# A two-layer graph network on Trainium2: row transfers in two parts of 67 and 61 rows, edge features from a 17-row copy, attributes in groups of prime size

## The chip, the cores and the metric

The kernel runs on one NeuronCore of a Trainium2 chip. The metric is device time in microseconds (us) of one execution, and lower is better. One execution was also profiled; engines are named as in the profile: PE is TensorE (matmuls), PEld its weight loads, DVE is VectorE, ACT is ScalarE, POOL is GpSimd, SP is SyncE.

## What is computed

There are 6250 nodes with 160 float32 features (64 scalars and 32 vectors of three components) and 200,000 edges, sorted by their destination node. Each of two layers gathers the features of every edge's source node, multiplies them with attributes of the edge (`edge_attr_4`, called `sh` in the kernel), sums the products by destination node, applies small dense weights to the sums, adds a residual and normalizes each node's row. Layer 1 also has a small network on ten further features of each edge (`edge_attr_10`, called `ea` in the kernel).

```python
def _L0_gnn_ref(x, sh, W1, ..., edge_index):
    ss, vv = (s[src], v[src])
    ...
    m = jnp.concatenate([out0, out1.reshape(-1, 3 * MUL1)], axis=1)
    m_agg = jax.ops.segment_sum(m, dst, num_segments=n)
    ...
    return x + jax.nn.relu(h)

def _L1_gnn_ref(node_input, node_attr, edge_src, edge_dst, edge_attr, edge_length_embedded, ...):
    h = jax.nn.relu(edge_length_embedded @ W_fc1 * (1.0 / np.sqrt(N_BASIS))) * RELU_GAIN
    w = h @ W_fc2 * (1.0 / np.sqrt(N_RADIAL))
    ...
    m0 = w0 * y0 * e0
    ...
    s0 = jax.ops.segment_sum(m0, edge_dst, num_segments=N) * inv
    ...
    return jnp.concatenate([out0, out1.reshape(N, 3 * MUL1)], axis=1)

x = _layernorm(x + _L0_gnn_ref(x, edge_attr_4, ...), axis=-1)
x = _layernorm(x + _L1_gnn_ref(x, node_vec1, src, dst, edge_attr_4, edge_attr_10, ...), axis=-1)
```

## The kernel before

The edges are cut into 391 chunks of 512 (`NCH`, `CH`), each four times 128 edges, and the nodes into 49 blocks of 128 (`NB`; the last has 106). `windowed` runs `sums` once for each layer. Since the edges are sorted, the destinations of one chunk lie in a narrow window of nodes (one window up to chunk 312, `HALF`; from there each chunk has two, one for either half of the partitions), and their sum is a small matmul into PSUM, added at the window's place in `acc`, an array in SBUF with a column for every node. The order of the chunks (`ORDER`, and its inverse `POS`) mixes those before and behind 312 in runs of eight and four.

The schedule is written out by hand, as a software pipeline. At step t each stage works on the chunk that stands `lag` places back in `ORDER`. The stages of layer 1, and then those of layer 0, are:

```python
stages = [(load, 0), (onehot, 1), (hidden, 1), (add, 4), (message, 2), (matmuls, 3)]
parts = [(fetch_base, 3), (project_last, 5), (residual_last, 6), (deviation, 7), (sent, 8)]
...
stages = [(load, 0), (onehot, 1), (add, 3), (matmuls, 2)]
```

- `load` issues four indirect DMAs of 128 rows on POOL (L206, `g<-in_x` in layer 0, `g<-ytab` in layer 1); a chunk's rows go into one of eight `g` buffers (`GRING`), and POOL waits until the matmuls of the chunk eight places earlier have read theirs. These are the gathers. Nothing else of weight runs on POOL.
- `load` also starts, in layer 1, the features of four chunks at every fourth chunk: two loads on SP (L342) of 10 rows each into partitions 0 to 9 and 64 to 73 of `et` or `early`, by turns. The `hidden` stage of the same chunk reads them one step later.
- The attributes come in groups of up to 32 chunks (`GROUPS`, 13 in each layer). Eight places before a group's first chunk, `attributes` issues four loads of up to 32 rows on SP into the tile `raw` (L368), one behind the other; where a group has fewer than 32 chunks, VectorE first sets `raw` to zero (L366). `turn` transposes the tile on VectorE (L374) at the group's first chunk. `raw` has one buffer.
- `onehot` compares each edge's destination with the window's nodes on VectorE (L381) and multiplies by the attributes into `S` (L385).
- In layer 1, `hidden` computes the network's hidden units (L394 on PE into `ph`, L397 on ACT into `h`), and `message` its outputs (L407 on PE into `pw`) and the products with the gathered rows (L410 and L415 on VectorE into `m`).
- `matmuls` multiplies `S` with the gathered rows, or with `m`, into `ab` in PSUM (L427); `add` transposes the result and adds it to `acc` on VectorE (L444 to L449).

When the last chunk of a node block is through (at position `CLOSE[b]`, at least three apart), the block's own steps follow, each some places later. In layer 0: `fetch` loads its rows of x (`xt`, SP, L486), `project` multiplies the sums with the weights (L461), `rectify` (`rl` on ACT, L497), `residual`, `deviation` (`sd` on ACT) and `normed` make the new rows, `turned`, `kept` (`xT` on ACT) and `linear` multiply them with layer 1's input weights, and `written` sends one result to `ytab` (ACT, L533), from which layer 1 gathers, and another to `btab` (SP, L537). In layer 1: `fetch_base` loads the block's rows of `btab` (`base`, SP, L486), and `project_last` (L548), `residual_last` (L553), `deviation` and `sent` finish it, the last with the write to `out` (SP, L559). All these transfers have 128 rows of 640 bytes, and go from SP or ScalarE; the gathers go from POOL through a queue of their own.

Of the kernel before, what the change touches and what calls it, by code (L numbers as in the profile page):

```python
# [18 lines left out]
P = 128  # L19
# [4 lines left out]
J = 4  # L24
# [20 lines left out]
PREPARE = 8  # L45

# [49 lines left out]
def floor_of(c):  # L96

    done = [b for b in range(NB) if CLOSE[b] < POS[c]]
    near = [b for b in done if (b >= LATE) == (c >= HALF)] or [b for b in done if b < LATE]
    return P * (max(near) + 1) if near else 0  # L100

# [110 lines left out]
def windowed(ctx: ExitStack, tc: tile.TileContext, x, srcs, rel, low, ident, iota, early, ahead, ea, sh, avec,  # L212
# [10 lines left out]
    btab = dram.tile([N, D], F32, name="btab")  # L223

# [87 lines left out]
    def sums(layer, table, gp, hp):  # L312
        with ExitStack() as s:
# [13 lines left out]
            def load(c):  # L327
                if layer or c not in ahead:
                    G[c] = gathered(nc, gp.tile([P, J, D], F32, name="g"), srcs, table, c)
                else:  # L330
                    G[c] = ahead.pop(c)
                if c % 4 == 0 and layer:

                    if POS[c] % 8 >= 4:
                        et = xp.tile([P, 2, CH], F32, name="et")
                    else:
                        et = early.rearrange("p a j d -> p (a j d)")
                        et = et[:, :2 * CH].rearrange("p (s e) -> p s e", s=2)
                    ET[c // 4] = et
                    for i in range(2):  # L340
                        if c + 4 <= NCH:
                            nc.sync.dma_start(et[64 * i:64 * i + 10, :, :],  # L342
                                              ea[:, c * CH:(c + 4) * CH].rearrange("f (s i e) -> f s i e", s=2, i=2)[:, :, i, :])
                        else:
                            for k in range(c + i, NCH, 2):
                                nc.sync.dma_start(et[64 * i:64 * i + 10, (k - c) // 2, :], ea[:, k * CH:(k + 1) * CH])
                for first, n in GROUPS:
                    if fetched[first] == POS[c]:
                        attributes(first, n)


            GROUPS = sorted(((a, min(32, end - a)) for begin, end in ((0, HALF), (HALF, NCH))
                             for a in range(begin, end, 32)), key=lambda g: POS[g[0]])
            fetched, last = {}, -2
            for first, n in GROUPS:
                fetched[first] = max(0, POS[first] - 8, last + 2)
                last = POS[first]

            def group(c):
                return c - (c - (c >= HALF) * HALF) % 32  # L360

            def attributes(first, n):

                raw = RAW[first] = hp.tile([P, 512], F32, name="raw")
                if n < 32:
                    nc.vector.memset(raw, 0.0)  # L366
                for q in range(4):
                    nc.sync.dma_start(raw[32 * q:32 * q + n, :],  # L368
                                      sh[first:first + n, 32 * q:32 * q + 32, :].rearrange("c p f -> c (p f)"))
# [6 lines left out]
            def onehot(c):  # L376
                if group(c) == c:
                    turn(c)
                w = width(c)
                oh = bank[:, :J * W].rearrange("p (j n) -> p j n", n=W)  # L380
                nc.vector.tensor_tensor(oh[:, :, :w], iota[:, None, :w].to_broadcast([P, J, w]),  # L381
                                        rel[:, c, :, None].to_broadcast([P, J, w]), op=ALU.is_equal)
                S[c] = ring[:, POS[c] % 3]
                attr = SH[group(c)][:, :, c - group(c)].rearrange("p (j k) -> p j k", j=J)
                nc.vector.tensor_tensor(S[c][:, :, :, :w], oh[:, :, None, :w].to_broadcast([P, J, 4, w]),  # L385
                                        attr[:, :, :, None].to_broadcast([P, J, 4, w]), op=ALU.mult)
# [68 lines left out]

            def projected(name, pool, weights, b):
                r = rows(b)
                po = T[name, b] = pool.tile([P, D], F32, name=name)
                for g in range(5):
                    lhs = acc[:, g, b * P:b * P + r]  # L460
                    nc.tensor.matmul(po[:r], lhs, weights[:, g, :], start=(g == 0), stop=(g == 4))  # L461
# [22 lines left out]
            def rows_of(name, table, b):  # L484
                t = T[name, b] = np_.tile([P, D], F32, name=name)
                nc.sync.dma_start(t[:rows(b)], table[b * P:b * P + rows(b), :])  # L486
# [41 lines left out]
            def written(b):  # L528
# [4 lines left out]
                nc.scalar.dma_start(ytab[b * P:b * P + r, :], y[:r])  # L533
# [3 lines left out]
                nc.sync.dma_start(btab[b * P:b * P + r, :], base[:r])  # L537
# [19 lines left out]
            def sent(b):  # L557
                normed("o", b)
                nc.sync.dma_start(out[b * P:b * P + rows(b), :], T.pop(("o", b))[:rows(b)])  # L559

            if layer:
                stages = [(load, 0), (onehot, 1), (hidden, 1), (add, 4), (message, 2), (matmuls, 3)]
# [5 lines left out]
            for t in range(max(CLOSE.values()) + 16):  # L568
                for f, lag in stages:
# [6 lines left out]
                if not layer:  # L576
                    for k in range(2 * t, min(2 * t + 2, 5)):
                        clear(k)
                if not layer and t == PREPARE:
# [394 lines left out]
```

## Time and profile before

| | |
|---|---|
| median of 4 runs | 4925.79 us |
| lowest and highest | 4915.60 and 4934.29 us |
| the profiled execution | 4930.84 us |
| its span (first to last instruction) | 4928.7 us |
| mean granted TensorE clock | 0.75 of full speed |
| PE busy | 2998.7 us, 61% |
| PEld busy | 2238.9 us, 45% |
| DVE busy | 2158.0 us, 44% |
| ACT busy | 376.0 us, 8% |
| POOL busy | 2965.7 us, 60% |
| gathers' queue (q0): packets, MB, share of 16 engines | 150144, 256.45, 19.5% |
| transfers from SP (q1) | 40702, 31.55, 2.2% |
| transfers from ScalarE (q10) | 7164, 4.80, 0.3% |

No engine is busy all the time. Layer 0 takes roughly the first 2264 us of the span, layer 1 the rest from about 2307 us; both have the same 391 chunks of four gathers, so the two layers take 1.43 and 1.65 us for each gather on average. The share of a queue is the time that its packets took, as a share of the time of 16 DMA engines, each with a ring of its own: 100% would be all 16 at work throughout. In a view of the instructions, a bracket or the last column gives the idle time just before, and after the arrow what ended it.

### The profile page before, as it was taken

What the parts mean: (1) busy time and instruction counts of PE and PEld (TensorE: products, weight loads), DVE (VectorE), ACT (ScalarE), POOL (GpSimd) and SP (SyncE); (2) the same over time, 40 slices, a digit from 0 to 9 for tenths busy, and PEclk for the clock granted to TensorE, in tenths of its full rate; (3) what the DMA queues carried; (4) which work ended last, traced back from release to release, by engine and by line L of the source; (5) the groups of instructions that cost most, each with busy time, mean ns of one, the idle gap of its engine ahead of it and who ended that gap; (6) DMA issues with size and microseconds to landing.
All of it is one profiled execution on the core that took longest, in us unless ns stands there. A gap on an engine that the chain in (4) does not pass through costs nothing.

```text
span 4928.7 us, 42324 instructions
## 1 busy us (share of the span) xinstructions
PE 2998.7 (61%) x12714; PEld 2238.9 (45%) x12715; DVE 2158.0 (44%) x6948; ACT 376.0 (8%) x747; POOL 2965.7 (60%) x3137
## 2 busy tenths in 40 slices
PE   2333433443444454455677877777777877778777
PEld 1333323333334343444455555555555555555555
DVE  3222222222323333333455555555555556556556
ACT  2000000000000000001000000000000001001000
POOL 5666666666666666664555555565555556555553
PEclk7656656666666666667788888888888888888888
DMA  2222222222222222222221222121222222222221
GB/s 65 64 57 58 62 64 64 60 66 62 68 64 66 63 68 64 68 70 55 57 57 53 59 57 57 54 62 53 57 61 56 59 59 62 59 54 60 57 58 38
DMA packets 198245, 295.60 MB, mean 60 GB/s; under 512 B 59270, under 2 KB 140668, under 8 KB 198010
## 3 DMA queue, kind: packets, MB, share of 16 engines
q0 software_dynamic: 150144, 256.45, 19.5%
q1 hardware_dynamic: 40702, 31.55, 2.2%
q10 hardware_dynamic: 7164, 4.80, 0.3%
q8 instruction: 107, 1.75, 0.1%
q14 instruction: 128, 1.05, 0.1%
HBM read 280.57 MB, written 12.00 MB: 59 GB/s over the span
## 4 chain that ended last, share of the span: by engine, by line
PE 39%; another core or an unknown queue 35%; DVE 13%; issue 10%; POOL 2%; ACT 1%; DMA 0%; DVEq 0%; ACTq 0%; SPq 0%; POOLq 0%
PE ab L427 22%; PE pw L407 10%; DVE m L415 3%; PE ph L394 3%; DVE S L385 3%; PE ph L461 2%; POOL g L206 2%; DVE acc L449 1%; DVE m L410 1%; PE bank L548 1%; DVE ab L447 1%; DVE ab L444 1%; DVE bank L381 1%; DVE ab L445 1%
## 5 line engine op out<-in xcount | busy, mean ns | idle before, releaser
L206 POOL DMA_INDIRECT g<-ytab,srcs x1564 | 1480.6, 947 | 1127.7 <-issue 441.6
L206 POOL DMA_INDIRECT g<-in_x,srcs x1556 | 1472.8, 947 | 761.1 <-issue 431.9
L427 PE MATMUL ab<-g,S 128*128 128x160 f32 (+1 forms) x3744 | 737.1, 399 | 818.9 <-issue 453.5
L427 PE MATMUL ab<-m,S 128*128 128x320 f32 (+1 forms) x3760 | 1094.2, 496 | 96.0 <-DVE acc L449 85.3
L427 PEld LDWEIGHTS ab<-g,S 128*128 128x128 f32 (+1 forms) x3744 | 655.2, 264 | 906.5 <-issue 465.6
L407 PE MATMUL pw<-fc,h 100*128 100x192 f32 x3128 | 733.0, 383 | 481.2 <-DVE m L415 376.7
L407 PEld LDWEIGHTS pw<-fc,h 100*128 100x128 f32 x3128 | 604.3, 221 | 713.9 <-issue 349.7
L427 PEld LDWEIGHTS ab<-m,S 128*128 128x128 f32 (+1 forms) x3760 | 700.0, 221 | 367.7 <-issue 200.8
L447 DVE STREAM_TRANSPOSE ab<-ab 128x160 f32<-128x160 f32 x470 | 169.4, 360 | 1301.2 <-remote 1036.3
L385 DVE TENSOR_TENSOR S<-bank,sh 128x384 f32<-128x384 f32 (+2 forms) x782 | 431.0, 551 | 642.3 <-remote 280.6
L415 DVE TENSOR_TENSOR m<-g,pw 128x192 f32<-128x192 f32 x1564 | 474.5, 344 | 0.0
L410 DVE TENSOR_TENSOR m<-pw,g 128x256 f32<-128x256 f32 x782 | 327.2, 418 | 287.8 <-remote 157.4
L397 ACT ACTIVATE h<-ph 100x512 f32<-100x512 f32 x391 | 229.7, 596 | 2278.5 <-remote 1054.0
L449 DVE TENSOR_TENSOR acc<-acc,ab 128x120 f32 (+2 forms) x940 | 261.4, 278 | 246.2 <-remote 130.9
L381 DVE TENSOR_TENSOR bank<-iota,rel 128x96 f32<-128x96 f32 (+2 forms) x782 | 199.2, 255 | 176.5 <-remote 82.8
L461 PE MATMUL ph<-wb,acc 128*128 128x160 f32 (+1 forms) x490 | 128.0, 436 | 242.7 <-DVE acc L449 140.8
L461 PEld LDWEIGHTS ph<-wb,acc 128*128 128x128 f32 (+1 forms) x490 | 111.9, 291 | 259.5 <-DVE acc L449 100.2
L445 DVE STREAM_TRANSPOSE ab<-ab 32x160 f32<-32x160 f32 x470 | 165.6, 352 | 16.2
L444 DVE STREAM_TRANSPOSE ab<-ab 128x160 f32<-128x160 f32 x470 | 167.1, 356 | 10.7 <-issue 5.8
L525 PE MATMUL pl<-wn,xT 128*128 128x320 f32 (+1 forms) x98 | 52.1, 622 | 136.2 <-issue 70.0
L394 PE MATMUL ph<-early,fc 10*100 10x512 f32 x392 | 118.9, 668 | 1.8 <-issue 1.7
L394 PE MATMUL ph<-et,fc 10*100 10x512 f32 x390 | 108.5, 628 | 1.2 <-issue 1.2
(80 smaller groups left out, 731.9 us busy)
## 6 DMA issues: line engine op xcount, KB each, us to landing
g<-ytab,srcs POOLq DMA_INDIRECT x1564
g<-in_x,srcs POOLq DMA_INDIRECT x1556
raw<-in_sh SPq DMA_DIRECT2D x88, 64.0 KB
early<-in_ea SPq DMA_DIRECT2D x98, 40.0 KB
xt<-in_x SPq DMA_DIRECT2D x48, 80.0 KB
ytab<-y ACTq DMA_DIRECT2D x48, 80.0 KB
btab<-base SPq DMA_DIRECT2D x48, 80.0 KB
et<-in_ea SPq DMA_DIRECT2D x96, 40.0 KB
```

Source lines behind the costliest of these rows:

```text
L206: nc.gpsimd.indirect_dma_start(out=g[:, j, :], out_offset=None, in_=table, in_offset=bass.IndirectOffsetOnAxis(ap=srcs[:, c, j:j + 1], axi ...
L381: nc.vector.tensor_tensor(oh[:, :, :w], iota[:, None, :w].to_broadcast([P, J, w]), rel[:, c, :, None].to_broadcast([P, J, w]), op=ALU.is_e ...
L385: nc.vector.tensor_tensor(S[c][:, :, :, :w], oh[:, :, None, :w].to_broadcast([P, J, 4, w]), attr[:, :, :, None].to_broadcast([P, J, 4, w]) ...
L394: nc.tensor.matmul(ph[:, i, :], fc1[g:g + 10, :], ET[c // 4][g:g + 10, c % 4 // 2, :], start=True, stop=True)
L397: nc.scalar.activation(H[c], H["p"][:, c % 2, :].rearrange("f (p j) -> f j p", j=J), AF.Relu, scale=FC_SCALE)
L407: nc.tensor.matmul(pw[:, j, :], h[:, q + j, :], fc2, start=True, stop=True)
L410: nc.vector.tensor_tensor(mq[:, :, :, 0:64], pw[:, :, 0:128].rearrange("p j (a u) -> p j a u", a=2), y[:, :, None, 0:64].to_broadcast([P, ...
L415: nc.vector.tensor_tensor(mq[:, :, a, 64:160].rearrange("p j (d u) -> p j d u", d=3), y1, pw[:, :, None, w:w + 32].to_broadcast([P, 2, 3, ...
L427: nc.tensor.matmul(ab[:, :n], one[h * i:h * i + h, j, :, :], t[h * i:h * i + h, j, :], start=(j == 0), stop=(j == J - 1), skip_group_check ...
L447: nc.vector.transpose(tr, blocks[:, 0])
L449: nc.vector.tensor_tensor(v, v, tr[:, :, :width(c)], op=ALU.add)
L461: nc.tensor.matmul(po[:r], lhs, weights[:, g, :], start=(g == 0), stop=(g == 4))
```

## The change

Most transfers of SP and ScalarE that run beside the gathers get a prime number of rows.

- The rows of a node block (`xt`, `base`, `btab`, `out` and `ytab`) are sent by a new helper, `sent_rows`, in two transfers, the first of 67 rows (`LEADS`) and the second of 61. The last block (106 rows) and the blocks that close within the last eight chunks keep one; 46 of 49 are split.
- The features are read from a copy in DRAM, `etab`, with 17 rows (`ROWS`): the ten of `ea` and the first seven again. Layer 0 makes it in eight stretches of the columns, each with two DRAM-to-DRAM transfers of 10 and 7 rows from SP, at its steps 32, 64 and so on to 256. Layer 1's loads bring all 17 rows into `et` (the matmuls still read ten of them), in a stage of its own that runs three chunks (`LEAD`) ahead of `load`.
- The attributes come in 15 groups of 31, 23, 19 or 17 chunks (`SIZES`). A group's four loads no longer follow each other but are issued one for each chunk, from twelve places ahead of its first chunk (or, where the group before is still in `raw`, as soon as that allows, then all at once if fewer than four places are left). Every group's `raw` is first set to zero.

```diff
--- before.py
+++ after.py
@@ -44,6 +44,12 @@
 GRING = 8
 PREPARE = 8
 
+LEADS = 67
+ROWS = 17
+SIZES = (31, 31, 31, 31, 31, 31, 23, 23, 23, 19, 19, 19, 31, 31, 17)
+COPIES = 8
+LEAD = 3
+
 
 def expected(node, sign):
 
@@ -98,6 +104,15 @@
     done = [b for b in range(NB) if CLOSE[b] < POS[c]]
     near = [b for b in done if (b >= LATE) == (c >= HALF)] or [b for b in done if b < LATE]
     return P * (max(near) + 1) if near else 0
+
+
+def group(c):
+
+    first = 0
+    for n in SIZES:
+        if c < first + n:
+            return first, n
+        first += n
 
 
 def windows(c):
@@ -221,6 +236,7 @@
     dram = ctx.enter_context(tc.tile_pool(name="dram", bufs=1, space=bass.MemoryType.DRAM))
     ytab = dram.tile([N, D], F32, name="ytab")
     btab = dram.tile([N, D], F32, name="btab")
+    etab = dram.tile([ROWS, NCH * CH], F32, name="etab")
 
     acc = const.tile([P, 5, NW], F32, name="acc")
     bank = ctx.enter_context(tc.tile_pool(name="bank", bufs=1, space=PSUM)).tile([P, 512], F32, name="bank")
@@ -329,44 +345,43 @@
                     G[c] = gathered(nc, gp.tile([P, J, D], F32, name="g"), srcs, table, c)
                 else:
                     G[c] = ahead.pop(c)
-                if c % 4 == 0 and layer:
-
-                    if POS[c] % 8 >= 4:
-                        et = xp.tile([P, 2, CH], F32, name="et")
+                for first, n in GROUPS:
+                    for q in range(4):
+                        if POS[c] == fetched[first] + (q if POS[first] >= fetched[first] + 4 else 0):
+                            attributes(first, n, q)
+
+            def features(c):
+                if c % 4:
+                    return
+
+                if POS[c] % 8 >= 4:
+                    et = xp.tile([P, 2, CH], F32, name="et")
+                else:
+                    et = early.rearrange("p a j d -> p (a j d)")
+                    et = et[:, :2 * CH].rearrange("p (s e) -> p s e", s=2)
+                ET[c // 4] = et
+                for i in range(2):
+                    if c + 4 <= NCH:
+                        nc.sync.dma_start(et[64 * i:64 * i + ROWS, :, :],
+                                          etab[:, c * CH:(c + 4) * CH].rearrange("f (s i e) -> f s i e", s=2, i=2)[:, :, i, :])
                     else:
-                        et = early.rearrange("p a j d -> p (a j d)")
-                        et = et[:, :2 * CH].rearrange("p (s e) -> p s e", s=2)
-                    ET[c // 4] = et
-                    for i in range(2):
-                        if c + 4 <= NCH:
-                            nc.sync.dma_start(et[64 * i:64 * i + 10, :, :],
-                                              ea[:, c * CH:(c + 4) * CH].rearrange("f (s i e) -> f s i e", s=2, i=2)[:, :, i, :])
-                        else:
-                            for k in range(c + i, NCH, 2):
-                                nc.sync.dma_start(et[64 * i:64 * i + 10, (k - c) // 2, :], ea[:, k * CH:(k + 1) * CH])
-                for first, n in GROUPS:
-                    if fetched[first] == POS[c]:
-                        attributes(first, n)
-
-
-            GROUPS = sorted(((a, min(32, end - a)) for begin, end in ((0, HALF), (HALF, NCH))
-                             for a in range(begin, end, 32)), key=lambda g: POS[g[0]])
+                        for k in range(c + i, NCH, 2):
+                            nc.sync.dma_start(et[64 * i:64 * i + ROWS, (k - c) // 2, :], etab[:, k * CH:(k + 1) * CH])
+
+
+            GROUPS = sorted({group(c) for c in range(NCH)}, key=lambda g: POS[g[0]])
             fetched, last = {}, -2
             for first, n in GROUPS:
-                fetched[first] = max(0, POS[first] - 8, last + 2)
+                fetched[first] = max(0, POS[first] - 12, last + 2)
                 last = POS[first]
 
-            def group(c):
-                return c - (c - (c >= HALF) * HALF) % 32
-
-            def attributes(first, n):
-
-                raw = RAW[first] = hp.tile([P, 512], F32, name="raw")
-                if n < 32:
-                    nc.vector.memset(raw, 0.0)
-                for q in range(4):
-                    nc.sync.dma_start(raw[32 * q:32 * q + n, :],
-                                      sh[first:first + n, 32 * q:32 * q + 32, :].rearrange("c p f -> c (p f)"))
+            def attributes(first, n, q):
+
+                if not q:
+                    RAW[first] = hp.tile([P, 512], F32, name="raw")
+                    nc.vector.memset(RAW[first], 0.0)
+                nc.sync.dma_start(RAW[first][32 * q:32 * q + n, :],
+                                  sh[first:first + n, 32 * q:32 * q + 32, :].rearrange("c p f -> c (p f)"))
 
             def turn(first):
 
@@ -374,14 +389,15 @@
                 nc.vector.transpose(sht, RAW.pop(first).rearrange("r (p f) -> r f p", f=16))
 
             def onehot(c):
-                if group(c) == c:
+                first = group(c)[0]
+                if first == c:
                     turn(c)
                 w = width(c)
                 oh = bank[:, :J * W].rearrange("p (j n) -> p j n", n=W)
                 nc.vector.tensor_tensor(oh[:, :, :w], iota[:, None, :w].to_broadcast([P, J, w]),
                                         rel[:, c, :, None].to_broadcast([P, J, w]), op=ALU.is_equal)
                 S[c] = ring[:, POS[c] % 3]
-                attr = SH[group(c)][:, :, c - group(c)].rearrange("p (j k) -> p j k", j=J)
+                attr = SH[first][:, :, c - first].rearrange("p (j k) -> p j k", j=J)
                 nc.vector.tensor_tensor(S[c][:, :, :, :w], oh[:, :, None, :w].to_broadcast([P, J, 4, w]),
                                         attr[:, :, :, None].to_broadcast([P, J, 4, w]), op=ALU.mult)
 
@@ -453,6 +469,13 @@
             def rows(b):
                 return min(P, N - b * P)
 
+            def sent_rows(engine, b, to, from_):
+
+                cut = LEADS if CLOSE[b] < NCH - 8 and rows(b) == P else rows(b)
+                for part in (slice(0, cut), slice(cut, rows(b))):
+                    if part.start < part.stop:
+                        engine.dma_start(to[part], from_[part])
+
             def projected(name, pool, weights, b):
                 r = rows(b)
                 po = T[name, b] = pool.tile([P, D], F32, name=name)
@@ -483,7 +506,7 @@
 
             def rows_of(name, table, b):
                 t = T[name, b] = np_.tile([P, D], F32, name=name)
-                nc.sync.dma_start(t[:rows(b)], table[b * P:b * P + rows(b), :])
+                sent_rows(nc.sync, b, t, table[b * P:b * P + rows(b), :])
 
             def fetch(b):
                 rows_of("xt", x, b)
@@ -530,11 +553,11 @@
                 pl = T.pop(("pl", b))
                 y = np_.tile([P, D], F32, name="y")
                 nc.scalar.activation(y[:r], pl[:r, 0:D], AF.Copy, scale=a_sb[:r, b:b + 1])
-                nc.scalar.dma_start(ytab[b * P:b * P + r, :], y[:r])
+                sent_rows(nc.scalar, b, ytab[b * P:b * P + r, :], y)
                 base = np_.tile([P, D], F32, name="base")
                 nc.vector.scalar_tensor_tensor(base[:r], pl[:r, D:2 * D], a_sb[:r, b:b + 1], T.pop(("x1", b))[:r],
                                                op0=ALU.mult, op1=ALU.add)
-                nc.sync.dma_start(btab[b * P:b * P + r, :], base[:r])
+                sent_rows(nc.sync, b, btab[b * P:b * P + r, :], base)
 
 
             def fetch_base(b):
@@ -556,16 +579,18 @@
 
             def sent(b):
                 normed("o", b)
-                nc.sync.dma_start(out[b * P:b * P + rows(b), :], T.pop(("o", b))[:rows(b)])
+                sent_rows(nc.sync, b, out[b * P:b * P + rows(b), :], T.pop(("o", b)))
 
             if layer:
-                stages = [(load, 0), (onehot, 1), (hidden, 1), (add, 4), (message, 2), (matmuls, 3)]
+                stages = [(load, 0), (features, -LEAD), (onehot, 1), (hidden, 1), (add, 4), (message, 2), (matmuls, 3)]
                 parts = [(fetch_base, 3), (project_last, 5), (residual_last, 6), (deviation, 7), (sent, 8)]
             else:
                 stages = [(load, 0), (onehot, 1), (add, 3), (matmuls, 2)]
                 parts = [(fetch, 4), (project, 6), (rectify, 7), (residual, 8), (deviation, 9),
                          (lambda b: normed("x1", b), 10), (turned, 11), (kept, 12), (linear, 13), (written, 14)]
             for t in range(max(CLOSE.values()) + 16):
+                if layer and not t:
+                    features(ORDER[0])
                 for f, lag in stages:
                     if 0 <= t - lag < NCH:
                         f(ORDER[t - lag])
@@ -576,6 +601,11 @@
                 if not layer:
                     for k in range(2 * t, min(2 * t + 2, 5)):
                         clear(k)
+                if not layer and t >= 2 * PREPARE and t % 32 == 0 and t // 32 <= COPIES:
+
+                    part = slice((t // 32 - 1) * (NCH * CH // COPIES), t // 32 * (NCH * CH // COPIES))
+                    nc.sync.dma_start(etab[0:10, part], ea[:, part])
+                    nc.sync.dma_start(etab[10:ROWS, part], ea[0:ROWS - 10, part])
                 if not layer and t == PREPARE:
                     prepare(up, pn)
```

## The prediction

> **What bounds the kernel now.** I read the page's groups of instructions first, to find the engine that sets the pace, and then stretches of the span without and with the transfers that the change touches.
>
> ```profile
> PE 39%; another core or an unknown queue 35%; DVE 13%; issue 10%; POOL 2%; ACT 1%; DMA 0%; DVEq 0%; ACTq 0%; SPq 0%; POOLq 0%
> ...
> L206 POOL DMA_INDIRECT g<-ytab,srcs x1564 | 1480.6, 947 | 1127.7 <-issue 441.6
> L206 POOL DMA_INDIRECT g<-in_x,srcs x1556 | 1472.8, 947 | 761.1 <-issue 431.9
> ```
>
> A gather takes POOL 0.947 us, and the idle time put down to "issue" is 0.28 us for each, so POOL can issue one per 1.25 us in the timeline, 5.0 us for a chunk of four. 3128 gathers would take 3910 us. The span is 4928.7 us: POOL also stood still for 761.1 - 431.9 = 329 us in layer 0 and 1127.7 - 441.6 = 686 us in layer 1. It waits there for TensorE to free one of the eight `g` buffers. The chain gives 35% to an unknown queue, so TensorE's own slowness does not explain it. One such stop in layer 1, in the timeline:
>
> ```profile
> 3999.96 0.37 SPq L559 DMA_DIRECT2D out<-z  x1
> 4000.43 1.27 SPq L342 DMA_DIRECT2D early<-in_ea  x2
> ...
> 4001.06 0.80 PE L427 MATMUL ab<-m,S 64*128 64x320 f32 x2
> ...
> 4005.57 0.95 POOL L206 DMA_INDIRECT g<-ytab,srcs  x1 [0.30 <-issue]
> 4008.98 0.56 DVE L385 TENSOR_TENSOR S<-bank,sh 128x384 f32<-128x384 f32 x1 [8.87 <-remote]
> ```
>
> VectorE waits 8.87 us for word that matmuls are done, though the last one shown starts at 4001.06. TensorE and VectorE stand still while POOL issues back to back until its buffers are used up (4006.52), and 2.46 us later VectorE goes on. The stops that end at 3614.11 and 3746.36 look alike, 2.39 and 2.50 us after POOL's last gather. So the pace is set by how late TensorE's finished matmuls become known while gathers are issued. SP's transfers stand just ahead of this stop; whether they cause it is what the change turns on, and the next table is the best witness:
>
> ```profile
> core 0: us, PE busy (x) PEld busy (x) DVE busy (x) ACT busy (x) POOL busy (x), PEclk, DMA share, GB/s
> 244.30:506.00 261.70, 94.07 (x426) 82.40 (x426) 57.90 (x196) 4.62 (x10) 172.50 (x183) 0.58 0.22 59
> ...
> 120.00:2264.00 2144.00, 920.95 (x4284) 775.50 (x4283) 618.92 (x1913) 93.63 (x262) 1416.78 (x1498) 0.63 0.24 64
> ```
>
> ```profile
> 3311.00:3372.00 61.00, 48.11 (x215) 33.52 (x213) 34.26 (x110) 5.85 (x11) 32.11 (x34) 0.86 0.18 50
> 4004.00:4061.00 57.00, 42.97 (x173) 29.82 (x173) 33.19 (x104) 4.96 (x9) 28.40 (x31) 0.79 0.18 47
> 2888.00:2946.00 58.00, 47.15 (x200) 32.48 (x200) 35.26 (x121) 6.04 (x11) 32.91 (x35) 0.82 0.19 50
> 2345.00:4860.00 2515.00, 1948.21 (x7806) 1368.86 (x7806) 1420.41 (x4607) 234.61 (x424) 1446.97 (x1529) 0.85 0.21 58
> ```
>
> Between 244.3 and 506.0 us SP and ScalarE issue nothing. The pace is 261.7 / 183 = 1.430 us per gather; over layer 0 it is 2144 / 1498 = 1.431. Layer 1 has shorter empty stretches: 1.79, 1.84 and 1.66 us, against 1.645 for the stage. Stretches without these transfers are no faster.
>
> **The change, part by part.** Sums are against the profiled run, 4930.84 us (2.1 us of it lie around the span); the median of the four runs, 4925.79, is 5 us lower.
>
> *Fewer rings per transfer.* The trace has no transfer on one ring, but one on two: the last block's `ytab` write has 106 rows, 2 x 53.
>
> ```profile
> q10 hardware_dynamic: 98, 0.06, 12.3%
> ```
>
> Between 2303.6 and 2305.5 us this queue's packets fill 12.3% of 16 engines, which is two rings. The Trainium skill (DMA: Bandwidth & Descriptors, "Why a DMA increments its semaphore by 16 and not by 1") says that a transfer runs on the largest number of rings up to 16 that divides its row counts; with it 67, 61, 31, 23, 19 and 17 rows each go to one ring. What one ring instead of sixteen saves is bounded from below by the empty stretches: nothing. From above I sort the 378 intervals between the last L427 matmuls of successive chunks in layer 1 by the transfers issued in the 3 us before they begin: 332 with none, mean 6.39 us; 19 with one, 7.43; 15 with two or three, 8.44; 12 with more, 8.38. That is 19 x 1.04 + 15 x 2.05 + 12 x 1.99 = 75 us. Sorted by transfers 6 to 10 us earlier, intervals are shorter by 50 us in sum; 10 to 16 us earlier, longer by 67. So up to 91 us, of which I take 45, the middle, since stops like the one above do follow such bursts.
>
> *Twice the issues.* 46 of 49 blocks send `xt`, `btab`, `base`, `out` and `ytab` in two parts: 184 more issues on SP at about 0.35 us, 64 us, and 46 on ScalarE at 0.326, 15 us. SP has nothing else to do. On ScalarE `rl`, `xT` and `sd` of later blocks stand behind them; ScalarE has 1% of the chain, so nothing, and 15 us if that cover goes.
>
> *Copies to `etab`.* Sixteen transfers in layer 0, eight times 17 rows of 100 kB. The page's queue q1 moved 31.55 MB in 2.2% of 16 x 4928.7 us, 55 us per MB of one ring: 5.5 us for a row, and 11 us on the rings that get one from both. Gathers on these rings queue behind. TensorE starts a chunk's matmuls 24.9 us (median, layer 0) after its last gather is issued, and eight gathers may be in flight, 10 us. Nothing, then; 8 x 11 = 88 us if that cover is gone.
>
> *Features three chunks ahead.* The matmuls that read them (L394) waited 1.8 and 1.2 us in all, so at most 3 us are to be had. The two loads of four chunks are 17 rows, 69.6 kB each now: 3.8 us each on a ring, 7.7 together, inside three chunks of 6.6 us.
>
> *Attributes in 15 groups, not 13, and a memset for each.*
>
> ```profile
> L374 DVE STREAM_TRANSPOSE sh<-raw 128x512 f32<-128x512 f32 x26 | 26.9, 1034 | 1.9 <-DMA raw<-in_sh 1.6 <-issue 0.3
> ...
> L366 DVE MEMSET raw<- 128x512 f32 x4 | 1.9, 485 | 0.2
> ```
>
> 26 more memsets at 0.485 us and 4 more transposes at 1.034 are 16.7 us on VectorE. By its 13% of the chain 2 us show, at most all 17; I take 5. The loads wait for the memset now, and SP behind them, 9 to 12 chunks ahead of use. The only wait here was 1.6 us.
>
> *A new queueing.* SP and ScalarE number their transfers over eight completion semaphores, and each waits for the landing of the one eight before it. On one ring a block's 82 kB take 4.5 us. In all, 36 MB plus 5.6 MB of padded features, less some 2 MB of start loads, are 40 MB: 2200 us of one ring's 4929, plus the gathers' 19.5%, 64%. I take nothing for it; its upper end is the rival below.
>
> Sum: -45 + 5, with 2 us of removed waits: about -40, so 4890 us.
>
> The same page (its table under "Rules for kernel authors") speaks against the change: it advises one transfer over all 128 partitions and 16 engines, and says of two halves that they gain nothing. By it the first term of the sum falls away, and 4934 remains.
>
> **The rivals.**
>
> *Ring 0 fills up (slower).* Ten blocks close at positions 343 to 382. In layer 0 these forty chunks bring 10 x 3 x 82 kB of rows, 135 us at 55 us per MB, 16 us of attributes, and 160 gathers at 0.307 (19.5% of 4928.7 over 3128): 200 us of the 230 that forty chunks take at 5.76. In layer 1 rows take 90, features 77, attributes 16, gathers 49: 232 of 264. From a price 15 to 20% above 55 us per MB the ring no longer keeps up, SP and ScalarE wait on landings, and `xt`, `base` and features come late. At 1.5 times it is 45 + 59 = 104 us: 5033. For it: both sums are close to full. Against: of the 106 rows above, 53 on each ring passed in 1.69 us (2303.72 to 2305.41 in the packets), 32 ns a row of 640 B, 50 us per MB.
>
> *The added work shows (slower).* VectorE's 17 us, ScalarE's 15 and part of the copies' 88: about +40, 4970. Against: each has its cover.
>
> *Nothing moves.* The empty stretches mean what they say: 4929. Here also belongs that rows are not confined to one ring.
>
> *The late word goes away altogether.* If any 16-ring transfer leaves the late state behind it, POOL's stops vanish in part; all 1015 us of them is the cap, half gives 4420. Against: 262 us without one changed nothing, and the start's 128-row loads keep their shape.
>
> **How the numbers follow.** Forecast (4840 to 4915): 0.43. Late word gone: 0.07. Nothing: 0.15. Ring 0: 0.20. Added work: 0.15. A measurement tells about 0.3%, 15 us, from no change. Faster: 0.40 of the forecast and the 0.07, 0.47; same: 0.15 and 0.03, 0.18; slower: 0.35. The range, 4790 to 5000, leaves out the 0.07 and half of ring 0's 0.20; the forecast's own is 4840 to 4915.
>
> **What would show it.** Right: intervals of layer 1 with transfers just ahead come down to 6.4 us, POOL's waits there fall by some 45 us, and layer 0 keeps 1.43 us per gather. A fall in layer 0 would refute the reading of the empty stretches. SP and ScalarE waiting on landings near the layers' ends, or L394 waiting for `etab` loads, would mean ring 0. Longer gathers in the eight copy stretches would mean the copies.

## The result, and the profile after

The changed kernel took 4931.38 us (median of 42 runs) where the kernel before took 4918.60 (63 runs beside them): a ratio of 1.0023, interval 1.0014 to 1.0031, or 11 us more with 7 to 15 as bounds. That is within the 0.3% named in the prediction, but it lies on the other side of the forecast of 4890. The profiled execution after took 4947.81 us with a span of 4946.1 us, 17 us more than the one before; single executions spread over some 30 us, so the size is taken from the medians and only the place from the trace.

The page after, its chain and the two groups of gathers:

```profile
PE 39%; another core or an unknown queue 35%; DVE 12%; issue 11%; POOL 1%; ACT 1%; DMA 1%; DVEq 0%; ACTq 0%; SPq 0%; POOLq 0%
...
L221 POOL DMA_INDIRECT g<-ytab,srcs x1564 | 1484.7, 949 | 1140.3 <-issue 487.2
L221 POOL DMA_INDIRECT g<-in_x,srcs x1556 | 1479.1, 951 | 754.7 <-issue 429.3
```

The stops have not moved: the unknown queue still has 35%, and POOL's idle time is 754.7 us in layer 0 (761.1 before) and 1140.3 in layer 1 (1127.7 before; the wait before its first gather, told of below, is 11.5 us of the difference). What the forecast wanted shorter is all there. So is the pattern it was taken from: the intervals of layer 1 that have transfers in the 3 us ahead of them are longer by some 80 us in sum, where it was 75.

The transfers did become what the change says. The queue of ScalarE while a block's `ytab` rows go out in parts of 67 and 61, from 2276.5 to 2279.5 us of the changed kernel:

```profile
DMA packets 74, 0.05 MB, mean 16 GB/s; under 512 B 1, under 2 KB 74, under 8 KB 74
...
q10 hardware_dynamic: 74, 0.05, 6.5%
```

6.5% of 16 engines is one ring (a sixteenth is 6.25%). Of the 74 packets one is a word of under 512 B, the one that follows the 67 rows; before, the same write ended with 16 such words, one from every ring. This is the rule of the Trainium skill that the prediction named (DMA: Bandwidth & Descriptors, "Why a DMA increments its semaphore by 16 and not by 1").

The loss stands where layer 0 ends. Layer 1's gathers wait for the last row of `ytab` (the view after names nothing that ended the wait, but the last packet of `ytab` is at 2317.40 us, just ahead of the gather). The timeline before, SP's issues and POOL's first gather of layer 1:

```profile
2291.00 0.33 SPq L537 DMA_DIRECT2D btab<-base  x1
2291.83 0.26 SPq L486 DMA_DIRECT2D xt<-in_x  x1
2294.25 9.37 SPq L537 DMA_DIRECT2D btab<-base  x4
...
2306.98 0.94 POOL L206 DMA_INDIRECT g<-ytab,srcs  x1 [42.09 <-DMA ytab<-y]
```

The same stretch after:

```profile
2292.29 0.88 SPq L477 DMA_DIRECT2D btab<-base  x2
2293.27 2.07 SPq L477 DMA_DIRECT2D xt<-in_x  x1
2295.61 19.61 SPq L477 DMA_DIRECT2D btab<-base  x5
...
2302.51 0.38 DVE L558 SCALAR_TENSOR_TENSOR base<-pl,a_sb,z 128x160 f32<-128x160 f32 x1 [4.07 <-DMA btab<-base]
2305.31 0.33 DVE L526 SCALAR_TENSOR_TENSOR z<-xt,rl 106x160 f32<-106x160 f32 x1 [2.42 <-DMA xt<-in_x]
...
2310.88 0.38 DVE L558 SCALAR_TENSOR_TENSOR base<-pl,a_sb,z 128x160 f32<-128x160 f32 x1 [3.74 <-DMA btab<-base]
...
2318.76 0.95 POOL L221 DMA_INDIRECT g<-ytab,srcs  x1 [53.56 <-issue]
```

Up to here the layers run level: the last gather of layer 0 starts at 2263.9 us before and at 2264.2 after. Then the first of layer 1 starts at 2306.98 and at 2318.76, so the gap grows from 43.0 to 54.5 us. No gathers run in it, and the blocks close one behind another as fast as their chain allows. The packets show one ring shared by two queues: from 2304 to 2306 us rows of SP's queue and of ScalarE's alternate, 35 of each, one every 28 ns, where ScalarE's queue alone (2279.4 to 2281 us) also sends one every 28 ns. So `ytab` and `btab` of the last two split blocks, 4 x 128 rows, take 14.4 us of that ring. `base` has two buffers, so VectorE waits for a `btab` write to land before it makes the next one (4.07 and 3.74 us), and it waits 2.42 us for the last `xt`. The four last `btab` writes, 9.37 us from first to last before, are five issues over 19.61 us after.

### The profile page after: what moved, and what is told of

Its sections match the earlier page's. It is cut to its first block, busy times and chain, and to the rows that moved or that the text cites. A ratio compares the mean times of both kernels' runs of the same rounds, so it can differ in the third digit from the quotient of the medians.

```text
span 4946.1 us, 42689 instructions
## 1 busy us (share of the span) xinstructions
PE 3013.6 (61%) x12714; PEld 2248.7 (45%) x12715; DVE 2174.8 (44%) x6978; ACT 375.5 (8%) x747; POOL 2976.1 (60%) x3137
## 4 chain that ended last, share of the span: by engine, by line
PE 39%; another core or an unknown queue 35%; DVE 12%; issue 11%; POOL 1%; ACT 1%; DMA 1%; DVEq 0%; ACTq 0%; SPq 0%; POOLq 0%
PE ab L443 23%; PE pw L423 9%; DVE m L431 3%; PE ph L410 2%; DVE S L401 2%; PE ph L484 2%; POOL g L221 1%; PE bank L571 1%; DVE acc L465 1%; DVE m L426 1%; DVE ab L460 1%; DVE ab L461 1%; DVE bank L397 1%; ACT h L413 1%
## 5 line engine op out<-in xcount | busy, mean ns | idle before, releaser
L221 POOL DMA_INDIRECT g<-ytab,srcs x1564 | 1484.7, 949 | 1140.3 <-issue 487.2
L221 POOL DMA_INDIRECT g<-in_x,srcs x1556 | 1479.1, 951 | 754.7 <-issue 429.3
L443 PE MATMUL ab<-g,S 128*128 128x160 f32 (+1 forms) x3744 | 755.4, 405 | 878.3 <-issue 526.5
L443 PEld LDWEIGHTS ab<-g,S 128*128 128x128 f32 (+1 forms) x3744 | 668.3, 269 | 971.9 <-issue 552.9
```

Of the source, the lines that this page charges most:

```text
L221: nc.gpsimd.indirect_dma_start(out=g[:, j, :], out_offset=None, in_=table, in_offset=bass.IndirectOffsetOnAxis(ap=srcs[:, c, j:j + 1], axi ...
L443: nc.tensor.matmul(ab[:, :n], one[h * i:h * i + h, j, :, :], t[h * i:h * i + h, j, :], start=(j == 0), stop=(j == J - 1), skip_group_check ...
```

## The experiments

Each ratio is against runs of the kernel before on the same chip, made beside it. Five batches were run, with the kernel before at 4875.95, 4876.87, 3981.21, 4875.56 and 4937.04 us. The third stands apart and has a section of its own. The profile before belongs to none of them (its runs have a median of 4918.60 us), so a pace or an idle time below is compared with other runs of the same batch where there are any.

### Where the loss is

```diff
-                cut = LEADS if CLOSE[b] < NCH - 8 and rows(b) == P else rows(b)
+                cut = LEADS if CLOSE[b] < NCH - 40 and rows(b) == P else rows(b)
```

> The changed kernel, with the blocks that close in the last 40 positions (not the last 8) sent whole, in both layers. Theory E (end of layer): the 12 us between the two medians come from the end of layer 0, where the halves of the last split blocks queue on one ring and POOL's first gather of layer 1 starts 11.8 us later (2318.8 against 2307.0 us); so that gather comes back to 2307 within 4 us, and the time to 0.999 to 1.001 of the kernel before. Rival S (spread): the loss is the sum of small costs all over the span (46 more issues on ScalarE, 26 more memsets, the copies); then it stays at 1.002 to 1.003. Rival C (cancelled): one ring saves some 45 us of stops, and added work takes them back; then this edit gives 12 us at most and says nothing more.

Measured: 4878.87 us, 1.0010 (0.9996 to 1.0023). The first gather of layer 1 stands 41.0 us behind the last of layer 0:

```profile
2289.14 0.94 POOL L221 DMA_INDIRECT g<-ytab,srcs  x1 [40.03 <-DMA ytab<-y]
```

The end theory holds for the gap; the interval does not exclude that a few us are left elsewhere.

The split alone, put into the kernel before:

```diff
+                cut = LEADS if CLOSE[b] < NCH - 8 and rows(b) == P else rows(b)
+                for part in (slice(0, cut), slice(cut, rows(b))):
+                    if part.start < part.stop:
+                        engine.dma_start(to[part], from_[part])
...
-                nc.sync.dma_start(t[:rows(b)], table[b * P:b * P + rows(b), :])
+                sent_rows(nc.sync, b, t, table[b * P:b * P + rows(b), :])
```

> The kernel before with nothing but the rows of the node blocks in 67 and 61. Theory E: the whole loss is here, 1.002 to 1.003, with the first gather of layer 1 10 to 13 us later than before. Rival S: a part of it, 1.0005 to 1.0015. Rival C: a gain, 0.990 to 0.998, since the transfers that stood ahead of stops are on one ring without the other parts' work.

Measured: 4894.91 us, 1.0037 (1.0023 to 1.0050), and the gap is 53.0 us. All of the loss is in the split. Of its 18 us (11 to 24) some 10 are at the boundary, and the interval leaves 1 to 14 elsewhere. The rest of the change without the split:

```diff
-LEADS = 67
+LEADS = 128
```

> The changed kernel with every block's rows in one transfer of 128 rows, as before; the copy, the features of 17 rows three chunks ahead and the attribute groups of prime size stay. If the twofold issues of the blocks are what the loss comes from (at the end of layer 0 and, by the run with 64 and 64 rows, 1.0029 with an undisturbed boundary, in the middle): 0.997 to 1.0005. If the copies, the memsets or the lead cost the rest: 1.001 to 1.003. Layer 1's first gather 43 us behind layer 0's last, within 3 us, in both.

Measured: 4879.36 us, 0.9997 (0.9980 to 1.0014), gap 44.0 us. The copy, the lead, the padded features, the memsets and the attribute groups together cost nothing that can be told, and gain nothing.

The changed kernel itself, once more and beside two runs told of below:

> The changed kernel itself, on the chip of these runs. At 1.42 to 1.65 us a gather: 1.001 to 1.004, the loss at the layer boundary. At 1.25 us a gather, where POOL sets the pace alone: the boundary costs the same 10 to 12 us, a larger share, and ring 0 is loaded a fifth more densely: 1.003 to 1.006; if it then fills up, above 1.01.

Measured: 4893.66 us, 1.0033 (1.0017 to 1.0049), gap 52.6 us, where the two neighbours that send the last blocks whole have 42.1 and 43.9. The loss repeats, and in the same place.

### Whether the transfers cause the stops

In layer 1 the features, attributes and `base` rows are loaded for the first chunks and used again, and only the last blocks reach the output:

```diff
+                        if POS[c] >= 8:
+                            continue
...
+                if layer and POS[first] >= 40:
+                    RAW[first] = KEPT["raw"]
+                    return
...
+                if layer and name in KEPT:
+                    T[name, b] = KEPT[name]
+                    return
...
+                if CLOSE[b] < NCH - 40:
+                    T.pop(("o", b))
+                    return
```

> The kernel before, with nearly all of layer 1's transfers from SP left out (features, attributes and base rows are loaded only for the first chunks and used again, and only the blocks of the last 40 positions are sent to the output): some 300 of 324 transfers less. If these transfers cause POOL's stops in layer 1, as the forecast assumed for 45 to 75 us: its pace falls from 1.645 to 1.61 us a gather or less, and the time to 4845 to 4875 (0.985 to 0.991). If they only stand beside them (theory N): 1.64 to 1.65 us a gather, and the time is within 10 us of before (0.998 to 1.001).

Measured: 4858.99 us, 0.9964 (0.9946 to 0.9981). SP issues 211 transfers instead of 531, and these 320 fewer are worth 18 us, 9 to 26. Neither time expected was met: more than nothing, and far less than the 75 us of the sort. The page of this kernel, SP's queue and the gathers:

```profile
q1 hardware_dynamic: 20650, 14.16, 1.0%
...
L206 POOL DMA_INDIRECT g<-ytab,srcs x1564 | 1480.1, 946 | 1075.3 <-issue 481.0
```

The kernel before was not profiled in this batch; the run with the last blocks whole was, and has all the transfers. Its gathers of layer 1:

```profile
L221 POOL DMA_INDIRECT g<-ytab,srcs x1564 | 1485.8, 950 | 1086.0 <-issue 431.6
```

POOL still stands idle for 1075.3 us in layer 1, against 1086.0. The pace is 1.611 us a gather, which meets the first theory's number, but only because this batch is faster throughout: the run with the last blocks whole has 1.624, and the difference of 0.012 us over 1564 gathers is 19 us, the gain in time once more. In this kernel and in the one before alike, just under 110 intervals of the layer (from one chunk's last product matmul to the next one's) are longer than 8 us. So nearly all of the stops come without the transfers.

### What one ring and more issues cost

The whole change in sizes that take 16 rings, but for the attribute groups of 8 and 15 chunks:

```diff
-LEADS = 67
-ROWS = 17
-SIZES = (31, 31, 31, 31, 31, 31, 23, 23, 23, 19, 19, 19, 31, 31, 17)
+LEADS = 64
+ROWS = 16
+SIZES = (32, 32, 32, 32, 32, 32, 32, 32, 16, 16, 16, 8, 32, 32, 15)
```

> The changed kernel with 64 and 64 rows, 16 rows of features and groups of 32, 16, 8 and 15 chunks: the same copies, lead, memsets and almost the same number of transfers, but nearly all over 16 or 8 rings. Theory E with no effect of the rings on POOL's stops: 0.998 to 1.001 of the kernel before, the layer boundary back within 4 us. Rival C: the saving of one ring is lost and the added work remains, 1.008 to 1.012. Rival S: 1.002 to 1.003, as the changed kernel.

Measured: 4887.08 us, 1.0029 (1.0015 to 1.0043), gap 43.4 us. The boundary is back, yet the loss is as large as the changed kernel's: theory E's time fails and rival S's number holds. But the work that S names is in the run with the last blocks whole too, at 1.0010, so S does not explain it either. It was run again:

> The run with 64 and 64 rows, 16 rows of features and groups of 32, 16, 8 and 15 again. A loss that repeats: 1.0015 to 1.0043. Chance, by the four parts of 32 rows that cost nothing (1.0001) and the other parts that cost nothing (0.9997): 0.998 to 1.001. At 1.25 us a gather: within 0.002 of 1.

Measured: 4944.52 us, 1.0021 (1.0004 to 1.0037), gap 44.6 us. The loss repeats, so it is hardly chance. And without the split, so with features and attributes alone on 16 rings (the same edit with `LEADS = 128`):

> The changed kernel with whole blocks, features of 16 rows and attribute groups of 32, 16, 8 and 15: the parts of the change other than the split, on 16 rings where the run with whole blocks had them on one. If features and attributes on 16 rings are what made the run with 64 and 64 rows 0.3% slower (so that one ring saves there): 1.0015 to 1.004. If that run's loss was the split or chance: 0.998 to 1.001. At 1.25 us a gather: within 0.002 of 1.

Measured: 4932.28 us, 0.9994 (0.9975 to 1.0013). Features and attributes cost the same on 16 rings as on one, nothing that can be told. So it is the two halves of 64 rows that cost some 10 us, and not between the layers: with halves, 16 rings are no cheaper than one (1.0023 and 1.0033 for the changed kernel), only the place differs.

To widen the difference between rings, the rows of the 39 blocks that close before position 351 were sent in four parts, the last blocks whole: 585 transfers more than before, on one ring each and then on 16.

```diff
+CUTS = (0, 37, 68, 99, 128)
...
+                cuts = CUTS if CLOSE[b] < NCH - 40 and rows(b) == P else (0, rows(b))
+                for part in map(slice, cuts, cuts[1:]):
+                    engine.dma_start(to[part], from_[part])
```

> As the run before it with four parts on one ring each (585 transfers more). On the chip of that run the gathers went at 1.25 us each and the kernel before took 3981 us, so POOL hid every transfer. Where the gathers go at 1.42 to 1.65 us (4876 to 4931 us): 1.000 to 1.004 if a transfer on one ring costs next to nothing, 1.004 to 1.010 if the number of issues costs, below 0.999 by the forecast's reading. At 1.25 us again: 1.0005 within 0.001.

Measured: 4893.57 us, 1.0045 (1.0029 to 1.0061). The other has `CUTS = (0, 32, 64, 96, 128)`:

> The same with four parts of 32 rows on 16 rings. Where the gathers go at 1.42 to 1.65 us: 1.004 to 1.010 by the run with 64 and 64 rows, and more than the four parts on one ring; 0.998 to 1.002 if shape and number are hidden. At 1.25 us: 1.000 within 0.001.

Measured: 4876.37 us, 1.0001 (0.9987 to 1.0014). The intervals do not touch. The same number of issues is free on 16 rings and costs 22 us (14 to 30) on one. SP's queue on the two pages, one ring first:

```profile
q1 hardware_dynamic: 38830, 31.54, 2.3%
```

```profile
q1 hardware_dynamic: 48190, 31.58, 2.5%
```

The difference of 9360 packets is 15 for each of the 624 parts that SP sends (39 blocks, four tables, four parts): a word from every ring instead of one. So fewer words do not pay. That slower landings are what costs is likely, but no run shows it. Where in the span the 22 us lie is not to be seen: the gap between the layers is 43.9 and 42.1 us, and the two profiled executions, 4891.69 and 4887.16 us, lie closer than the medians. Why halves of 64 rows cost something that quarters of 32 do not is open too; the quarters stop 40 positions before the end, the halves eight, and that may be it, but halves with whole last blocks were not tried on 16 rings.

### What the pace does depend on

The number of `g` buffers, six for eight:

> The kernel before with six g buffers, not eight. Theory W (late word): TensorE's word comes late for as long as POOL issues without a break, so POOL stops when its buffers are used up, whatever SP does; with six buffers it stops sooner and more often, the 99 stops of layer 0 become 130 or more and the time 1.02 to 1.05. Rival P (plain pace): TensorE and VectorE need 5.7 us for a chunk on average and the stops are only where POOL waits for them; then the ring's size changes nothing, 0.998 to 1.003.

Measured: 4853.88 us, 0.9953 (0.9934 to 0.9972). Fewer buffers are faster. With twelve in layer 0 (eight, and four from a pool of their own):

> The kernel before with twelve g buffers in layer 0 (eight and four more from a pool of their own), eight in layer 1. Theory W: fewer stops in layer 0, 270 us of them become 130 to 200, the time 0.970 to 0.988, with layer 1 as before. Rival P: 0.998 to 1.002.

Measured: 4879.09 us, 0.9997 (0.9978 to 1.0016), gap 48.9 us. And a pause on POOL after each chunk:

```diff
                     G[c] = gathered(nc, gp.tile([P, J, D], F32, name="g"), srcs, table, c)
+                    nc.gpsimd.memset(rest, 0.0)
```

> The kernel before with a small memset on POOL after each chunk's four gathers, a pause of 0.1 to 0.3 us every 5 us. Theory W with words that come in any gap: the stops shrink by more than the 782 pauses cost, 0.97 to 0.995. Theory W with words that need some 2.4 us of silence: the pauses are added to POOL's own time and the stops shrink by about as much or less, 0.998 to 1.02. Rival P: the stops shrink by just the pauses, 0.998 to 1.002.

Measured: 4881.30 us, 1.0013 (0.9995 to 1.0031). The page has the memset and the idle time that made room for it:

```profile
L206 POOL DMA_INDIRECT g<-ytab,srcs x1564 | 1487.6, 951 | 1026.9 <-issue 410.0
L206 POOL DMA_INDIRECT g<-in_x,srcs x1556 | 1480.2, 951 | 690.4 <-issue 404.4
L331 POOL MEMSET rest<- 128x16 f32 x780 | 102.6, 131 | 0.2
```

Between the twentieth gather and the last of layer 0 the pace is 1.426 us a gather with six buffers, 1.424 with twelve and 1.427 with the pause. POOL stands idle there for over 0.6 us 92 times with six buffers and 89 times with twelve, where it was 99 before. Theory W, which expected 130 or more with six, falls; something else sets 1.43 us, and POOL's stops are where it waits for that. What six buffers gain is at the ends: the gap between the layers is 36.5 us (43.0 with eight, 48.9 with twelve) and the time from the last gather to the end 44.6 us (56.5), together 18 of the 23 us. The likely reason is that POOL runs less far ahead, so less is left behind its last gather. Rival P did not name the ends. Four buffers go on in the same way:

> The kernel before with four g buffers again. At 1.42 to 1.65 us a gather: 0.987 to 0.993 if the pace is fixed and only the ends shrink, 1.01 or more if four buffers are too few there. At 1.25 us: 1.002 within 0.001.

Measured: 4850.36 us, 0.9953 (0.9937 to 0.9968). The gap is 28.7 us and the end 37.4, yet the time is no better than with six. The profiled execution has a slower layer 1 (1.640 us a gather against 1.618 with six), but it took 4874.12 us, 24 more than the median, so it does not show where the gain went. Fewer buffers are the one edit that beats both kernels with nothing left out, by 0.5%.

### The batch at 3981 us

> The kernel before with four g buffers, not eight. The pace of the gathers did not depend on the ring's size (six: 1.426 and 1.618 us a gather, eight: 1.42 to 1.43 and 1.61 to 1.65), and with six the ends were shorter: 36.5 us between the layers instead of 43 to 44, and 44.6 us from the last gather to the end instead of 56.5. Theory F (fixed pace): both ends shrink by as much again, some 7 and 12 us, twice that at most, the pace stays within 0.3%: 0.987 to 0.993 of the kernel before. Rival: four buffers are too few to bridge the late words, the pace falls: 1.01 to 1.06.

> The kernel before with three g buffers. Theory F: as four or 5 us better, 0.984 to 0.993. Rival: with the products reading a chunk two to three steps after its load, three buffers leave POOL nothing to run ahead with, and each chunk waits for its gathers: 1.03 to 1.15. The two together show where the ring begins to matter.

> The kernel before with the rows of the 39 blocks that close before position 351 sent in four transfers of 37, 31, 31 and 29 rows, one ring each: 585 transfers more, the ends of the layers as before. If a transfer on one ring costs next to nothing (by the run with the last blocks whole, +3 us for some 240 more): 1.000 to 1.004. If the number of issues is what costs: as the run with four times 32 rows, 1.004 to 1.010. Forecast's reading (one ring takes stops away): below 0.999.

> The same four transfers of 32 rows each, which take 16 rings. By the run with 64 and 64 rows (1.0029 for some 250 more transfers, 0.03 to 0.085 us each): 585 more cost 18 to 50 us, 1.004 to 1.010. If the transfers are hidden whatever their shape: 0.998 to 1.002, as with one ring.

In this batch the kernel before took 3981.21 us (28 runs, 3979.05 to 3983.42). Against it: four buffers 1.0020 (1.0011 to 1.0029), three 1.0033 (1.0021 to 1.0045), four parts on one ring 1.0005 (0.9996 to 1.0014), four parts on 16 rings 1.0001 (0.9992 to 1.0010). The page of the last one:

```profile
POOL 29%; issue 22%; DMA 20%; PE 17%; DVE 10%; ACT 1%; SPq 0%; DVEq 0%; ACTq 0%; POOLq 0%
...
L208 POOL DMA_INDIRECT g<-ytab,srcs x1564 | 1480.6, 947 | 498.6 <-issue 408.8
L208 POOL DMA_INDIRECT g<-in_x,srcs x1556 | 1472.3, 946 | 475.2 <-issue 399.4
```

The unknown queue is gone from the chain, POOL leads it, and, but for the first gathers of layer 0, POOL is nowhere idle for over 0.6 us within a layer: 1.251 us a gather in both layers, the rate that the prediction read as POOL's own. Where the words come in time POOL sets the pace, the shape and number of the transfers are hidden, and the ends are short already (23.4 us between the layers), so a smaller ring has nothing to gain there. None of these four tells the theories of the slower pace apart; two were therefore repeated above, as was the ring of four.

## Why the prediction was wrong

**Fewer rings per transfer, -45 us: the step that failed.** "So up to 91 us, of which I take 45, the middle, since stops like the one above do follow such bursts." The sort of intervals showed which transfers stand ahead of long ones, and was read as what they cost. Leaving nearly all of layer 1's transfers out gave 18 us (9 to 26), not 75, so confining them to one ring had no 45 us to take. After the change the sort gives some 80 us again, and among the runs above it gives from some 40 us (whole blocks) to over 160 (the split alone) at times within 0.4% of each other. A likely reason, argued and not shown: SP's issues wait for the same words of TensorE and VectorE that the stops wait for, so a late word puts both beside each other. The lower bound, nothing, from the stretches without transfers, was nearer. The sign was wrong as well where the transfers were cut in four: that costs 22 us on one ring and nothing on 16. The page's rule that spoke against the change (the Trainium skill, DMA: Bandwidth & Descriptors, "Rules for kernel authors": one transfer of 128 partitions, since halves gain nothing) gave 4934 with the sum's other terms, and the runs side with it: no split was faster than whole blocks. That 4934 lies so near the measured 4931 is luck, since the sum starts from an execution of 4930.84 us and the kernel before has a median of 4918.60.

**A new queueing, nothing: mis-sized.** "I take nothing for it; its upper end is the rival below." It cost some 10 us, in one place: at the end of layer 0, where no gathers run, VectorE waits for landings and layer 1 waits for the last block. The prediction summed the ring's load over forty chunks and did not look at the stretch where the rows of a few blocks are nearly all that is on the way and the next layer waits for the last of them. There two queues on one ring got a row every 28 ns between them, not each.

**Twice the issues, nothing.** Right by the four parts of 32 rows. The two halves of 64 rows contradict it by some 10 us, and that is not settled.

**Copies, features, attributes and memsets, +5 - 2 us.** 0.9997 and 0.9994 without the split: right, within 10 us.

**The rivals.** Of *Ring 0 fills up* the waits came where it said, near the end of a layer, but only of layer 0, and for a tenth of its 104 us. *The added work shows* did not come. *Nothing moves* is the nearest case: the pace is untouched, and the boundary makes most of the 11 us (its number, 4929, is near for the same lucky reason). *The late word goes away* did not come, though the third batch shows what it would be worth: 3981 us. The time stayed inside the range of 4790 to 5000; 0.40 of the 0.47 for faster rested on a term that no run shows.

## What to carry to other kernels

A sort of long intervals by what stood ahead of them prices nothing where both may hang on the same late event; leave the suspect out for one run before building a change on it. A slow transfer costs most surely where somebody waits for its landing, so look at the end of a phase, where the next one waits for the last row; four parts on one ring, which leave these ends alone, cost nothing at 3981 us and 22 us at 4876, in a place that was not found. And where POOL does not set the pace, a deep ring of buffers did not speed it up and lengthened what was left at the end: six and four buffers were faster than eight, though at 3981 us four and three were 0.2 and 0.3% slower.

## What was not expected of the hardware

The same program ran at two paces: 4876 to 4937 us in four of the five batches and 3981 us in one. The batches of 3981 and of 4937 us name the same chip number, so the number does not tell them apart. What differs in the profile is the unknown queue, with 31 to 36% of the chain at the slower pace (20% with four buffers) and none at the faster. The granted clock differs too. The run with four parts on 16 rings at 3981 us, layer 0 and layer 1:

```profile
core 0: us, PE busy (x) PEld busy (x) DVE busy (x) ACT busy (x) POOL busy (x), PEclk, DMA share, GB/s
120.00:1800.00 1680.00, 1246.06 (x3798) 783.67 (x3797) 564.45 (x1711) 80.96 (x225) 1270.55 (x1345) 0.56 0.30 73
2100.00:3800.00 1700.00, 1561.19 (x7014) 1060.65 (x7013) 1291.06 (x4135) 211.85 (x378) 1286.29 (x1359) 0.98 0.31 76
```

In layer 1 the clock is 0.98, where it was 0.85 in the prediction's table; in layer 0 it is lower, 0.56 for 0.63, and the layer is faster all the same. So layer 0 is not slow for want of clock. Nor do TensorE and VectorE need the 5.7 us for a chunk that rival P took as theirs: here four gathers, and so a chunk, take 5.0 us. At the slower pace a gather took 1.42 to 1.44 us in layer 0 whether POOL had six, eight or twelve buffers, with pauses of 131 ns and without them; what sets that number was not found.
